# A two-layer graph network on one core: the prologue written in program order, and the softmax's reductions moved from TensorE to GpSimd

## The chip, the cores and the metric

One Trainium2 chip, one of its cores. The metric is device time in microseconds (us). On one core every run quoted here was in the fast state (mean granted TensorE clock 0.989 or more); only such runs are compared. The profiled execution's own length, the span, is some 2 us shorter than the time of the same run.

## The reference, cut to what matters

There are 32 batches of 512 nodes with 512 features, all float32.

```python
for each batch:
    h  = relu(layernorm(x))                      # layer 0
    a  = adj / max(rowsum(adj), 1e-6)
    x1 = x + relu(concat(h, a @ h) @ W.T)
    h1 = relu(layernorm(x1))                     # layer 1
    q, k = split(h1 @ Wqk);  v = h1 @ Wv
    w  = mask * rowsum(q * (adj @ (k * mask))) / sqrt(512)
    out = x1 + softmax(w over the 512 nodes)[:, None] * v
```

The softmax is over nodes, and the nodes lie on the 128 partitions (four to each), so its maximum and its sum need a reduction over partitions.

## The kernel before: the parts that the argument touches

All large products are one generator of seven block products (a Strassen scheme): each step is one group of eight matmuls of 128x256 on line 124. The names are used throughout: `y` is h times half of W, `o` the rest of layer 0, `t`, `u`, `v` the products of layer 1. A batch has 42 such groups. A group's results leave the PSUM through a copy on ScalarE and sums on VectorE. A right-hand matrix must be transposed: the rows go out to DRAM, come back exchanged in blocks (`saT`, `shT` are the tiles read back), and VectorE turns 32x32 blocks (`STREAM_TRANSPOSE`). Every engine runs its own list in order.

```python
class Softmax:                       # before; one per batch
    def maximum(self):
        ptop = ps_s.tile([1, P], F32, ...)
        nc.tensor.transpose(ptop, self.top, identity)          # over partitions, on TensorE
        nc.vector.tensor_reduce(self.ntop, ptop, AX.X, ALU.max, negate=True)
    def exponents(self):
        pbc = ps_s.tile([P, 1], F32, ...)
        nc.tensor.matmul(pbc, ones[0:1, :], self.ntop, ...)    # back to all partitions
        nc.vector.tensor_copy(self.nbc, pbc)
        nc.scalar.activation(self.e, self.w, AF.Exp, bias=self.nbc)
    def weights(self):
        psum = ps_s.tile([P, 1], F32, ...)
        nc.tensor.matmul(psum, ones, self.es, ...)             # sum over partitions
        nc.vector.reciprocal(self.rs, psum)
        ...
# the prologue: left to the scheduler, one thing after another
front_h(0)                            # batch 0: layernorm, h written to DRAM
weight_right(w0[:, F:2 * F], w2R, "w2")
turn_all(FH[0].to)                    # read back, turned on VectorE
front_a(0)                            # adj likewise
run(SINGLE[:7], [layer0_y(0)], {})
weight_right(w0[:, 0:F], w1R, "w1")
turn_all(FA[0].to)
load_x(0)                             # x of batch 0 a second time
multiply, keep = layer1_weights()     # wq, wk, wv
front_h(1); front_a(1); masks()
... # cut
with tc.manual_schedule(...):         # from here on in program order
    for i in range(B + 1):
        ...
```

Of the kernel before, what the change touches and what calls it, by code (L numbers as in the profile page):

```python
# [9 lines left out]

F32 = mybir.dt.float32
AF = mybir.ActivationFunctionType
ALU = mybir.AluOpType
# [8 lines left out]
def kernel(  # L22
# [45 lines left out]
    ps_m = ctx.enter_context(tc.tile_pool(name="ps_m", bufs=7, space=bass.MemoryType.PSUM))  # L68
    ps_s = ctx.enter_context(tc.tile_pool(name="ps_s", bufs=1, space=bass.MemoryType.PSUM))
# [117 lines left out]
    def exchange(src, name):  # L187


        t = big.tile([P, 8, P], F32, tag="s", bufs=2, name=name)  # L190
        for q in range(Q):
            nc.sync.dma_start(out=t[q * R:(q + 1) * R, :, :], in_=src[:, :, ts(q, P)].rearrange("k r j -> r k j"))
        return t
# [7 lines left out]
    ones = const.tile([P, P], F32, name="ones")  # L201
    nc.vector.memset(ones, 1.0)
# [202 lines left out]
    class Softmax:  # L405
        def __init__(self, b):
            self.b = b
            self.w = small.tile([P, C], F32, tag="w", name=f"w_{b}")
            self.e = small.tile([P, C], F32, tag="e", name=f"e_{b}")
            self.sm = small.tile([P, C], F32, tag="sm", name=f"sm_{b}")  # L410
            for n, shape in (("top", [P, 1]), ("ntop", [1, 1]), ("nbc", [P, 1]), ("es", [P, 1]), ("rs", [P, 1])):
                setattr(self, n, small.tile(shape, F32, tag=n, name=f"{n}_{b}"))
# [8 lines left out]
        def maximum(self):  # L421
            ptop = ps_s.tile([1, P], F32, tag="s", name=f"ptop_{self.b}")
            nc.tensor.transpose(ptop, self.top, identity)
            nc.vector.tensor_reduce(self.ntop, ptop, AX.X, ALU.max, negate=True)

        def exponents(self):
            pbc = ps_s.tile([P, 1], F32, tag="s", name=f"pbc_{self.b}")
            nc.tensor.matmul(pbc, ones[0:1, :], self.ntop, start=True, stop=True)  # L428
            nc.vector.tensor_copy(self.nbc, pbc)
            nc.scalar.activation(self.e, self.w, AF.Exp, bias=self.nbc)  # L430

        def row_sum(self):
            nc.vector.tensor_reduce(self.es, self.e, AX.X, ALU.add)

        def weights(self):
            psum = ps_s.tile([P, 1], F32, tag="s", name=f"psum_{self.b}")
            nc.tensor.matmul(psum, ones, self.es, start=True, stop=True)
            nc.vector.reciprocal(self.rs, psum)
            nc.vector.tensor_scalar(self.sm, self.e, self.rs, None, op0=ALU.mult)
# [17 lines left out]
    def weight_right(src, dst, name):  # L457

        s = src.rearrange("(h k r) j -> h k r j", h=2, r=R)
        for h in range(2):  # L460
            t = exchange(s[h], f"s{name}_{h}")
            for k in range(2):
                nc.vector.transpose(  # L463
                    dst[:, 2 * k + h, :, :].rearrange("p b (k r) -> p k b r", r=R),
                    t[:, :, ts(k, 2 * R)].rearrange("p k (c r) -> p k c r", r=R),
                )
        for s in right_sums(dst):
            s()

    def weight_rows(src, dst, ordered, name):  # L470


        s = src.rearrange("(h k r) j -> h k r j", h=2, r=R)
        for h in range(2):
            t = exchange(s[h], f"s{name}_{h}").rearrange("p k (a r) -> p k a r", r=R)
            if ordered:
                for q in range(2):
                    o = dst.rearrange("p a (c q r) -> p q c a r", c=C, q=Q)[:, 2 * h + q]
                    nc.vector.transpose(o, t[:, q * 4:(q + 1) * 4, :, :])
            else:  # L480
                nc.vector.transpose(dst[:, :, ts(h, H)].rearrange("p a (k r) -> p k a r", r=R), t)
# [4 lines left out]
    def masks():  # L486
        t = big.tile([P, C, 512], F32, tag="u", bufs=1, name="masks")
        mask_sb = t[:B, 0, :]
        nc.sync.dma_start(out=mask_sb, in_=nodemask)
        mask_by = t[:B, 1, :]  # L490
        nc.vector.tensor_copy(
            mask_by.rearrange("b (c q r) -> b c q r", c=C, q=Q), mask_sb.rearrange("b (q c r) -> b c q r", q=Q, c=C)
        )
        pmk = ps_s.tile([P, C, B], F32, tag="s", name="pmk")
        for c in range(C):
            nc.tensor.transpose(pmk[:, c, :], mask_by[:, ts(c, P)], identity[:B, :B])
        nc.scalar.activation(mcol, pmk, AF.Copy, scale=scale)
        nc.scalar.activation(mraw, pmk, AF.Copy)

    def layer1_weights():  # L500

        wqT = big.tile([P, C, 512], F32, tag="u", bufs=1, name="wqT")
        wkT = slots("h1T", 1, "wkT")[:, 0:4, :, :].rearrange("p s b f -> p (s b f)").rearrange("p (c f) -> p c f", c=C)
        weight_rows(wqk[:, 0:F], wqT, True, "wq")
        weight_rows(wqk[:, F:2 * F], wkT, False, "wk")
        tv = big.tile([P, C, 512], F32, tag="v", bufs=1, name="tv")
        load_rows(tv, wv)
        for c in range(C):
            nc.scalar.activation(
                vR[:, 2 * (c // 2):2 * (c // 2) + 2, c % 2, :],  # L510
                tv[:, c, :].rearrange("p (a f) -> p a f", a=2), AF.Copy,
            )
        for s in right_sums(vR):
            s()
        held = {}

        def multiply(d):
            p = held[d] = mm_tile(f"pm_{d}")
            for a in range(C):
                nc.tensor.matmul(  # L520
                    p.rearrange("p a f -> p (a f)"), wqT[:, a, ts(d, P)], wkT[:, a, :],
                    start=(a == 0), stop=(a == C - 1),
                )

        def keep(d):
            copy(mR[:, 2 * (d // 2):2 * (d // 2) + 2, d % 2, :], held[d])

        return multiply, keep

    FH, FA, F1 = {}, {}, {}  # L530

    def front_h(b):
        f = FH[b] = FrontH(b)
        f.load(0)
        f.load(1)
        for c in range(C):
            f.stats(c)
        variance(f.t)
        shift(f.t)
        for c in range(C):  # L540
            f.write(c)

    def front_a(b):
        f = FA[b] = FrontA(b)
        for h in range(2):
            f.load(h)
            f.sum(2 * h)
            f.sum(2 * h + 1)
            f.degrees(h)
            f.write(2 * h)  # L550
            f.write(2 * h + 1)

    def turn_all(t):
        for h in range(2):
            t.read(h)
            t.turn(h)
        for i in range(4):
            t.sums(i)

    front_h(0)  # L560
    weight_right(w0[:, F:2 * F], w2R, "w2")
    turn_all(FH[0].to)
    front_a(0)
    run(SINGLE[:7], [layer0_y(0)], {})
    weight_right(w0[:, 0:F], w1R, "w1")
    turn_all(FA[0].to)
    load_x(0)
    multiply, keep = layer1_weights()
    front_h(1)
    front_a(1)  # L570
    masks()
    for h in range(2):
        FA[1].to.read(h)
    if B > 2:
        FH[2] = FrontH(2)
        FH[2].load(0)
        FH[2].load(1)


    with tc.manual_schedule(  # L580
        engines={mybir.EngineType.PE, mybir.EngineType.Activation, mybir.EngineType.DVE, mybir.EngineType.SP}
    ):
        for i in range(B + 1):
# [5 lines left out]
            if i + 1 < B:  # L589
                ta, th = FA[i + 1].to, FH[i + 1].to  # L590
                at(1, ta.turn, 0)
                at(3, ta.turn, 1)
                at(3, th.read, 0)
                at(5, th.read, 1)
                for k in range(4):
                    at(4 + k, ta.sums, k)
# [12 lines left out]
            if i == 0:  # L609
                for d in range(C):  # L610
                    at(3 * d, multiply, d)
                    at(3 * d + 3, keep, d)
                for k in range(4):
                    at(13, right_sums(mR)[k])
# [24 lines left out]
            if i == B:  # L639
# [4 lines left out]
                PAIR if i < B else sorted(PAIR),  # L644
                [layer1_t(i - 1), layer1_v(i - 1)] if i > 0 else [None, None], plan,
# [9 lines left out]
            if i > 0:  # L655
                s = Softmax(i - 1)
                for n, f in ((0, s.scores), (1, s.maximum), (2, s.exponents), (3, s.row_sum), (4, s.weights)):
                    at(n, f)
                for c in range(C):
                    at(5 + c, s.apply, c)  # L660
                at(6, s.store, 0)
                at(8, s.store, 1)
# [49 lines left out]
```

## Time and profile before

| | before |
|---|---|
| time, median of the runs beside the changed kernel | 2452.25 us (2450.97 to 2453.15, 4 runs) |
| span of the profiled run | 2448.9 us |
| TensorE idle before 154 us | 69 us |
| period of a batch | 73.36 us |

From the page of the kernel before, the busy shares and the chain of work that ended last:

```profile
PE 2372.5 (97%) x10948; PEld 2070.0 (85%) x10948; DVE 1501.6 (61%) x3169; ACT 852.8 (35%) x1547; POOL 65.4 (3%) x70
PE 94%; DMA 2%; DVE 1%; ACT 1%; SPq 1%; issue 0%; POOL 0%; DVEq 0%; ACTq 0%; POOLq 0%
```

Busy and chain agree that TensorE sets the end. The TensorE timeline (start, us, engine, line, operation, out<-in; in brackets the idle time before and what ended it) shows the large idle stretches of the prologue:

```profile
23.75 3.78 PE L124 MATMUL pp_y<-w2R,hT 128*128 128x256 f32 x8 [23.75 <-DVE hT L198]
48.98 3.78 PE L124 MATMUL pp_o<-w1R,hT 128*128 128x256 f32 x8 [8.85 <-DVE w1R L463]
55.86 3.78 PE L124 MATMUL pp_o<-y,aT 128*128 128x256 f32 x8 [3.10 <-DVE aT L198]
100.00 0.60 PE L496 MATMUL pmk<-identity,masks 32*128 32x32 f32 x4 [4.91 <-DVE masks L491]
125.83 3.75 PE L124 MATMUL pp_y<-w2R,hT 128*128 128x256 f32 x8 [25.22 <-DVE rstd L227]
```

Batch 0 waits for its round trip through DRAM, then for w1, for the mask, and batch 1 for a normalization that begins only when all else has gone. A first group after a long gap takes 3.75 to 3.78 us instead of 1.89: this is called the cold clock below (in the stretch from 100 to 120 us the profile's granted TensorE clock is 0.50 of full speed).

### The profile page before, as it was taken

The numbers are of one execution on the slowest core, as the hardware profiler recorded it, in microseconds if no ns is written. First come the engines' busy times: TensorE is split into PE (matmuls) and PEld (weight loads), VectorE is DVE, ScalarE is ACT, GpSimd is POOL, SyncE is SP. The second block draws the span as 40 slices with busy tenths as digits, with TensorE's granted clock in tenths as the row PEclk, the third lists the DMA queues.
The fourth block names the chain that finished last, engine by engine and source line by source line (L and its number), as shares of the span: only waits on it lengthen the run. The fifth ranks groups of instructions, "written<-read, shape, count | busy, mean of one in ns | idle before, by whom it ended". The sixth has DMA issues, their size and how long they took to land.

```text
span 2448.9 us, 30843 instructions
## 1 busy us (share of the span) xinstructions
PE 2372.5 (97%) x10948; PEld 2070.0 (85%) x10948; DVE 1501.6 (61%) x3169; ACT 852.8 (35%) x1547; POOL 65.4 (3%) x70
## 2 busy tenths in 40 slices
PE   3599999999999999999999999999999999999998
PEld 3378888888888888888888888888888888888887
DVE  4466666666666666666666666666666666665544
ACT  2233433323433323433323433323333323333322
POOL 0000000000000000000000000000000000000000
PEclk8899999999999999999999999999999999999999
DMA  6765545655545755555656555656545655645512
GB/s 157 179 181 138 144 124 145 168 143 138 145 126 143 172 138 138 146 128 140 172 138 138 147 128 138 173 138 138 155 123 137 172 138 138 154 126 134 121 40 65
DMA packets 369930, 342.94 MB, mean 140 GB/s; under 512 B 33360, under 2 KB 270928, under 8 KB 369776
## 3 DMA queue, kind: packets, MB, share of 16 engines
q1 hardware_dynamic: 369776, 340.99, 56.2%
q8 instruction: 85, 1.39, 0.2%
q14 instruction: 69, 0.57, 0.1%
HBM read 206.64 MB, written 134.22 MB: 139 GB/s over the span
## 4 chain that ended last, share of the span: by engine, by line
PE 94%; DMA 2%; DVE 1%; ACT 1%; SPq 1%; issue 0%; POOL 0%; DVEq 0%; ACTq 0%; POOLq 0%
PE pp_o L124 17%; PE pp_y L124 9%; PE pp_t L124 9%; PE pp_u L124 9%; PE pp_v L124 9%; PE pq_o L124 9%; PE pq_y L124 5%; PE pq_t L124 5%; PE pq_u L124 5%; PE pq_v L124 4%; PE pr_o L124 4%; PE pr_u L124 2%; PE pr_t L124 2%; PE pr_v L124 2%; PE pr_y L124 2%; PE pbc L428 0%
## 5 line engine op out<-in xcount | busy, mean ns | idle before, releaser
L124 PE MATMUL pp_y<-w2R,hT 128*128 128x256 f32 x1024 | 249.0, 387 | 50.3 <-DVE rstd L227 25.2
L124 PEld LDWEIGHTS pp_y<-w2R,hT 128*128 128x128 f32 x1024 | 194.0, 192 | 77.1 <-issue 25.3
L124 PE MATMUL pp_o<-w1R,hT 128*128 128x256 f32 x1024 | 243.8, 381 | 8.8 <-DVE w1R L463 8.8
L124 PE MATMUL pp_o<-y,aT 128*128 128x256 f32 x1024 | 243.8, 381 | 3.1 <-DVE aT L198 3.1
L124 PE MATMUL pp_u<-h1m,aT 128*128 128x256 f32 x1024 | 242.4, 380 | 0.1
L124 PE MATMUL pp_v<-vR,h1T 128*128 128x256 f32 x1024 | 242.1, 379 | 0.0
L124 PE MATMUL pp_t<-mR,h1T 128*128 128x256 f32 x1024 | 241.9, 379 | 0.0
L124 PEld LDWEIGHTS pp_o<-w1R,hT 128*128 128x128 f32 x1024 | 195.7, 191 | 35.9 <-DVE w1R L463 9.2
L124 PEld LDWEIGHTS pp_o<-y,aT 128*128 128x128 f32 x1024 | 195.8, 191 | 30.4 <-DVE aT L198 3.8
L124 PEld LDWEIGHTS pp_t<-mR,h1T 128*128 128x128 f32 x1024 | 194.7, 190 | 26.3
L124 PEld LDWEIGHTS pp_u<-h1m,aT 128*128 128x128 f32 x1024 | 192.1, 190 | 29.2 <-ACT h1m L332 0.7
L124 PEld LDWEIGHTS pp_v<-vR,h1T 128*128 128x128 f32 x1024 | 194.6, 190 | 26.2
L91 ACT ACTIVATE o<-pp_o 128x512 f32<-128x512 f32 x96 | 57.3, 597 | 397.6 <-PE pp_o L124 397.6
L198 DVE STREAM_TRANSPOSE aT<-saT 128x1024 f32<-128x1024 f32 x64 | 79.7, 1245 | 151.0 <-DMA saT<-daT 141.2
L236 ACT ACTIVATE h1m<-x,nmr,rstd 128x512 f32<-128x512 f32 x128 | 100.0, 807 | 170.7 <-DVE nmr L232 170.7
L91 ACT ACTIVATE v<-pp_v 128x512 f32<-128x512 f32 x128 | 75.4, 589 | 223.6 <-PE pp_v L124 223.6
L91 ACT ACTIVATE y<-pp_y 128x512 f32<-128x512 f32 x128 | 75.8, 592 | 214.6 <-PE pp_y L124 214.6
L228 POOL TENSOR_TENSOR rstd<-rstd,mhalf 128x4 f32<-128x4 f32 x64 | 64.7, 1011 | 2318.2 <-ACT m_o L91 1187.8
L124 PE MATMUL pq_y<-w2R,hT 128*128 128x256 f32 x512 | 123.7, 384 | 1.5 <-DVE hT L85 1.5
L124 PE MATMUL pq_v<-vR,h1T 128*128 128x256 f32 x512 | 121.0, 379 | 0.0
L124 PE MATMUL pq_o<-w1R,hT 128*128 128x256 f32 x512 | 121.0, 379 | 0.0
L124 PE MATMUL pq_t<-mR,h1T 128*128 128x256 f32 x512 | 121.0, 379 | 0.0
(113 smaller groups left out, 3722.4 us busy)
## 6 DMA issues: line engine op xcount, KB each, us to landing
n<-in_x_dram SPq DMA_DIRECT2D x256, 128.0 KB, 4.8
dhT<-n SPq DMA_DIRECT2D x128, 256.0 KB, 2.1
shT<-dhT SPq DMA_DIRECT2D x256, 128.0 KB, 4.5
a<-in_adj_dram SPq DMA_DIRECT2D x256, 128.0 KB, 3.1
daT<-a SPq DMA_DIRECT2D x128, 256.0 KB, 2.5
saT<-daT SPq DMA_DIRECT2D x256, 128.0 KB, 4.5
x<-in_x_dram SPq DMA_DIRECT2D x128, 256.0 KB, 5.6
dh1T<-h1m SPq DMA_DIRECT2D x128, 256.0 KB, 2.4
```

The lines of the kernel that those rows point to most:

```text
L91: nc.scalar.activation(o, i, AF.Copy)
L124: nc.tensor.matmul(p[:, rc, :], lt[:, LEFT[k], dk, ts(rc, P)], rt[:, RIGHT[k], dk, :], start=first and n == 0, stop=True, skip_group_check ...
L198: nc.vector.transpose(o, t.rearrange("p k (c r) -> p k c r", r=R))
L228: nc.gpsimd.tensor_tensor(rstd, rstd, mhalf, op=ALU.pow)
L236: nc.scalar.activation(o, i, AF.Relu, scale=t[1][:, c:c + 1], bias=t[2][:, c:c + 1])
```

## The change

Its intent: (1) write the prologue in program order as well, load x once and the weights early into tiles that are still free, and transpose batch 0 on TensorE, which has nothing else to do there, instead of through DRAM; (2) do the softmax's two reductions on GpSimd, so that TensorE's stream has no small products in it, and give the freed PSUM bank to the large products. The diff, cut to its core:

```diff
-    ps_m = ...tile_pool(name="ps_m", bufs=7, space=PSUM)
-    ps_s = ...tile_pool(name="ps_s", bufs=1, space=PSUM)
+    ps_m = ...tile_pool(name="ps_m", bufs=8, space=PSUM)
 class Softmax:
     def maximum(self):
-        nc.tensor.transpose(ptop, self.top, identity)
-        nc.vector.tensor_reduce(self.ntop, ptop, AX.X, ALU.max, negate=True)
+        nc.gpsimd.partition_all_reduce(self.gtop, self.top, channels=P, reduce_op=ReduceOp.max)
     def exponents(self):
-        nc.tensor.matmul(pbc, ones[0:1, :], self.ntop, start=True, stop=True)
-        nc.vector.tensor_copy(self.nbc, pbc)
-        nc.scalar.activation(self.e, self.w, AF.Exp, bias=self.nbc)
+        nc.vector.tensor_scalar(self.ntop, self.gtop, -1.0, None, op0=ALU.mult)
+        nc.scalar.activation(self.e, self.w, AF.Exp, bias=self.ntop)
     def row_sum(self):
         nc.vector.tensor_reduce(self.es, self.e, AX.X, ALU.add)
+        nc.gpsimd.partition_all_reduce(self.gs, self.es, channels=P, reduce_op=ReduceOp.add)
     def weights(self):
-        nc.tensor.matmul(psum, ones, self.es, start=True, stop=True)
-        nc.vector.reciprocal(self.rs, psum)
+        nc.vector.reciprocal(self.rs, self.gs)
+def start():                                     # all of it in program order
+    load_x(0)
+    s2 = [exchange(... w2 half h ..., queue=nc.scalar) for h in range(2)]
+    fa.load(0); fa.load(1)                       # adj of batch 0
+    s1 = exchange(... w1 ..., whole("v", "sw1")) # tiles that are free until layer 1
+    fh.load(0)                                   # x of batch 1
+    sq = exchange(... wq ..., whole("u", "swq")); sk = exchange(... wk ..., slot_rows("h1m", "swk"))
+    ... statistics of x ...
+    for c in range(C):
+        normalize into v
+        turn_chunk(v, c, "h")                    # four 128x128 transposes on TensorE
+        keep_chunk(h0, c - 1, "h")               # copied out by ScalarE
+    run(SINGLE[:7], [layer0_y(0)], plan)         # adj's chunks are turned between its groups
+    run(SINGLE, [layer0_out(0)], later)
+    run(SINGLE, [None], plan)                    # the q-k weight product
+    run(PAIR, [layer0_y(1), layer1_u(0)], plan)
... # cut: positions of the steps in these plans
 with tc.manual_schedule(engines=engines):
-    for i in range(B + 1):
+    start()
+    for i in range(1, B + 1):
... # cut: for i == 1, adj of batch 2 and the sums of three right-hand matrices lie in o(1)
```

## The prediction

> **What bounds the kernel now.** I read first the page's busy shares and its chain of work that ended last: TensorE is busy 97% of the span and 94% of the chain is TensorE. So time can only be won where TensorE is idle, or where it does work that could go elsewhere. To find the idle time I asked for the busy time of each engine in stretches, cut at the points where the TensorE timeline shows a gap. Columns: stretch, its length, then busy time (and count) of TensorE matmuls, weight loads, VectorE, ScalarE, GpSimd, then granted clock, DMA share, GB/s.
>
> ```profile
> 0.00:23.75 23.75, 0.00 (x0) 0.00 (x0) 9.74 (x21) 4.21 (x5) 1.72 (x7) 1.00 0.76 181
> 23.75:40.13 16.38, 14.67 (x56) 11.62 (x56) 7.11 (x12) 4.71 (x10) 0.00 (x0) 1.00 0.32 80
> 40.13:81.19 41.06, 29.12 (x113) 24.38 (x113) 18.27 (x27) 7.84 (x15) 0.00 (x0) 0.79 0.90 193
> 81.19:125.83 44.64, 14.51 (x38) 6.43 (x36) 23.16 (x52) 12.12 (x23) 2.31 (x3) 0.70 0.68 181
> 125.83:153.83 28.00, 26.79 (x113) 22.52 (x114) 20.47 (x34) 16.63 (x32) 0.98 (x1) 0.93 0.65 180
> 153.83:2441.71 2287.88, 2287.40 (x10633) 2005.11 (x10631) 1420.73 (x3024) 806.72 (x1461) 60.40 (x60) 1.00 0.56 138
> ```
>
> Idle TensorE is 23.75 + 1.71 + 11.94 + 30.13 + 1.21 = 69 us, all before 154 us; from there to 2441.71 it never stops, at full clock, and 7 us follow it for the last store. The DMA share and GB/s of the first stretches (181 to 193 GB/s) also say that the prologue moves data nearly as fast as this kernel ever does; that matters below.
>
> In the steady part a busy TensorE is not all useful. The timeline of TensorE (start, duration, line, out<-in, count) over one softmax:
>
> ```profile
> 350.62 1.89 PE L124 MATMUL pr_y<-w2R,hT 128*128 128x256 f32 x8
> 352.35 0.27 PE L423 MATMUL ptop<-identity,top 128*1 128x128 f32 x1
> 352.45 1.89 PE L124 MATMUL pp_u<-h1m,aT 128*128 128x256 f32 x8
> 354.28 0.38 PE L428 MATMUL pbc<-ntop,ones 1*128 1x1 f32 x2
> 354.58 1.99 PE L124 MATMUL pp_y<-w2R,hT 128*128 128x256 f32 x8
> 356.42 1.89 PE L124 MATMUL pr_u<-h1m,aT 128*128 128x256 f32 x8
> 358.14 0.28 PE L437 MATMUL psum<-es,ones 128*128 128x1 f32 x2
> 358.28 1.97 PE L124 MATMUL pq_y<-w2R,hT 128*128 128x256 f32 x8
> 360.09 1.89 PE L124 MATMUL pp_u<-h1m,aT 128*128 128x256 f32 x8
> ```
>
> Undisturbed groups of eight start every 1.727 us. Here five groups take 360.09 - 350.62 = 9.47 us where 8.64 would do: the three small softmax products cost 0.83 us, mostly as breaks in the stream, not as their own duration. A second reading: the GpSimd pow of line 228 recurs every 388.60 - 315.24 = 73.36 us, while the 42 groups of a batch are 42 x 1.727 = 72.53. Both give 0.83 us a batch, and say that nothing else stops TensorE there.
>
> **What the Trainium skill says.** (1) "TensorE: Matmul & The Clock Gate", part 1, § What's actually happening: after an idle window the array runs at half clock until about 3.4 us of activity. The trace agrees: the first group after each gap takes 3.78 us in place of 1.89, so each closed gap is worth some 1.8 us more. (2) "GPSIMD Engine Reference", § 4 names GpSimd for reductions over partitions, but § 2.1 says the first call to a freshly loaded kernel pays about 6 us of code load. The order of the changed kernel shows a library instruction on GpSimd before each pair of reductions and another before the next pow; no run here shows their cost yet. (3) The same page, § 3.2, times a partition reduction of 128x2048 at 247.7 us, 0.12 us a column, so on one column only the fixed cost counts. The trace has no such instruction; its nearest, pow on 128x4, takes 1.01 us. (4) "DMA: Bandwidth & Descriptors", § Issuing engines are not separate DMA queues: ScalarE's queue shares the sixteen DMA engines with SyncE's, so the second queue for w2 adds no bandwidth. No run here shows that yet.
>
> **Part 1, softmax (steady).** Removed: 0.83 us of TensorE on each of 32 batches = 26.5 us, all on the path. Added: two reductions on GpSimd, off TensorE, but VectorE's negation and reciprocal, and ScalarE's exponential, wait for them in order. How long may one take, D? Before, in the batch at 422 us, the row maximum was ready at 422.84; nbc began at 428.05 and the reciprocal at 431.82:
>
> ```profile
> 422.68 0.16 DVE L419 TENSOR_REDUCE top<-w 128x1 f32<-128x4 f32 x1
> 428.05 0.16 DVE L429 COPY nbc<-pbc 128x1 f32<-128x1 f32 x1 [1.76 <-PE pbc L428]
> 431.82 0.17 DVE L438 RECIPROCAL rs<-psum 128x1 f32<-128x1 f32 x1 [1.54 <-PE psum L437]
> ```
>
> So VectorE already waited 5.2 us for the maximum and 9.0 us for the sum, since the products stood at fixed places in TensorE's order, and TensorE lost nothing by it. The new chain is D, negate and exponential and row sum (about 0.8), D: with 2D + 0.8 below 9.0, D under 4.1 us, it is never later than before. Estimate from pow: D is 1.5 to 4 us. The library instructions have no wait and stand right after a pow, some 22 us ahead of the maximum (13 groups), so I take them as hidden. Part 1: -26.5 us. The eighth PSUM bank gains nothing, as TensorE did not wait for banks.
>
> **Part 2, prologue.** Batch 0 of h and adj no longer goes through DRAM and back; x is loaded once; the weights' loads are issued early into tiles that are free. I walk TensorE's new order with durations of the trace.
> - Start: 1 MB of x and 1 MB of w2 share the DMA; at 190 GB/s x is complete at about 10 us (before, without w2 ahead: 7.4). Statistics 3.0, pow with its neighbours 1.4: 14.5. ScalarE then does four normalizations of 0.73 and the copies of the transposed chunks at 0.6; the last transposition is ready near 20. y(0) starts at 20, not 23.75.
> - y(0): seven groups 12.1, cold start 1.8, twelve transposes of adj at about 0.2 (a weight load of 0.19 each) 2.4: ends at 36.5, with w1 landed by 25.
> - o(0): 14 x 1.727 = 24.2, four transposes and the mask 1.2: ends at 62. Before, o(0) waited 8.85 us for w1R and 3.10 for aT.
> - The q-k weight product: 13.9 as before, its inputs landed by 40: ends at 76.
> - y(1) with u(0): hT of batch 1 must be turned by 76. Its loads end at 40, ScalarE writes it out at 54 to 58, wv's 1 MB lies in the queue between, it is read back by 68 to 70. It just fits, hidden by the weight product. So the stage begins near 76, not 125.83, and warm: it takes 24.2 plus some 2 us waiting for ScalarE (masks of h1m), so o(1) begins at about 102, not 153.83: 51 us won.
> - But then DMA traffic that before had 154 us must go in 110. Up to the half of aT(2) that VectorE wants early in o(1), I count 20.5 MiB (x of batches 0 and 1: 2; five weight blocks: 5; adj of batch 0: 1; h and adj of batches 1 and 2, loaded: 4, written out: 3.5, read back so far: 2.5; h1 of batch 0, out and back: 2; half of h 3: 0.5); at 190 to 215 GB/s that is 100 to 113 us plus the gaps. I allow 7 us of new waits in o(1) and the stage after. Part 2: -44 us.
>
> The tail is a wash: the last sum needs about 2D + 1.9 us after the last maximum, before it took 9.8.
>
> Sum: 2451.5 - 26.5 - 44 = 2381.
>
> **The rivals.** (a) A reduction that is slow or whose library load falls between maximum and exponential. Each us of D above about 5.5 then holds up ScalarE's PSUM copies and costs one to two us a batch; with 6 us of load in each batch I estimate 0.7 to 2 us a batch, 2405 to 2445, and D near 10 makes it slower than before by 100 us or more. For it: two library instructions a batch. Against it: the early position, and the 0.08 us between identity's memset and its select in the kernel before, which also has a library instruction between. (b) DMA bounds the new prologue: not 7 but 15 to 25 us of TensorE waits in the first 150 us, since VectorE runs in order and one late turn blocks the finishes behind it. Result 2390 to 2400. For it: 190 GB/s already. Against it: the plan moves some turns of batch 2 later, as if to allow for it. (c) Hardly any new wait: 2372.
>
> **Range and chances.** Faster by over 2% means under 2402.5. The middle case, (b) and (c) all stay under; only (a) reaches above it. I give (a) 13%, a fifth of that slower than 2%. So 2381, 2366 to 2408; faster 0.86, same 0.11, slower 0.03.
>
> **What would show it.** Right: pow recurs every 72.5 us in the profile after; TensorE's idle time before the first y(1) product is 20 to 25 us and that product starts at 74 to 80; o(1) ends by 135; the reductions show 1.5 to 4 us from the row maximum to the negation. Wrong: a period of 73.4 or more (part 1 fails), with ScalarE waiting for ntop longest; long idle TensorE in o(1) with VectorE waiting for saT or x (part 2 mis-sized); y(0) starting past 25 because x waited behind w2.

## The result, and the profile after

| | before | after |
|---|---|---|
| time, median | 2452.25 us (4 runs) | 2382.84 us (2381.87 to 2383.87, 4 runs) |
| ratio of fast runs | | 0.9717, 95% interval 0.9701 to 0.9734 |
| span | 2448.9 us | 2380.0 us |
| period of a batch | 73.36 us | 72.52 us |
| start of y(1) | 125.83 us | 75.24 us |
| start of y(2) | 202.17 us | 161.10 us |

Here and below, a ratio is the mean time of one kernel's fast runs over the mean of the other's in the same rounds, so it is not quite the ratio of the medians quoted. The result is correct.

The page of the kernel after, busy shares:

```profile
PE 2345.8 (99%) x10820; PEld 2056.2 (86%) x10820; DVE 1491.9 (63%) x3132; ACT 860.3 (36%) x1555; POOL 91.9 (4%) x134
```

The same cut into stretches as the prediction made for the kernel before (length, then busy time of TensorE, weight loads, VectorE, ScalarE, GpSimd; granted clock, DMA share, which as the tool counts it can pass 1, GB/s):

```profile
0.00:21.83 21.83, 4.00 (x16) 3.20 (x17) 7.81 (x18) 5.88 (x8) 1.74 (x7) 1.00 1.05 189
21.83:102.89 81.06, 77.85 (x334) 61.79 (x334) 55.32 (x103) 41.15 (x79) 3.03 (x3) 1.00 0.83 189
102.89:161.10 58.21, 51.95 (x225) 44.28 (x224) 40.09 (x85) 17.58 (x31) 2.29 (x2) 0.94 0.57 155
161.10:2373.12 2212.02, 2212.02 (x10249) 1946.93 (x10247) 1386.79 (x2927) 795.13 (x1436) 84.87 (x122) 1.00 0.55 139
2373.12:2380.00 6.88, 0.00 (x1) 0.00 (x0) 1.87 (x3) 0.60 (x1) 0.00 (x0) 0.70 0.57 152
```

TensorE is now idle 17.8 us at the start and about 9.5 us between 97 and 147 us, and never again up to 2373.12. The gaps that are left, in the TensorE timeline after:

```profile
75.24 1.89 PE L124 MATMUL pp_y<-w2R,hT 128*128 128x256 f32 x8
101.06 1.99 PE L124 MATMUL pp_u<-h1m,aT 128*128 128x256 f32 x8 [3.21 <-ACT u L91]
137.80 3.78 PE L124 MATMUL pp_t<-mR,h1T 128*128 128x256 f32 x8 [4.63 <-ACT t L91]
147.18 1.99 PE L124 MATMUL pp_v<-vR,h1T 128*128 128x256 f32 x8 [1.13 <-ACT v L91]
```

y(1) starts with no wait and on a warm clock, where it had waited 25.22 us. The new gaps all wait for a copy on ScalarE. What that copy waited for is one step back on ScalarE, whose list holds the normalization of batch 3 (`n`) just ahead of the copy of `t`:

```profile
134.34 2.93 ACT L235 ACTIVATE n<-n,nmr,rstd 128x512 f32<-128x512 f32 x4 [12.63 <-DVE nmr L231]
137.17 0.57 ACT L91 ACTIVATE t<-pp_t 128x512 f32<-128x512 f32 x1
```

and `nmr` is computed by VectorE, which had stood still twice in that stage for the halves of batch 2's adj:

```profile
113.30 1.25 DVE L199 STREAM_TRANSPOSE aT<-saT 128x1024 f32<-128x1024 f32 x1 [7.36 <-DMA saT<-daT]
126.07 1.25 DVE L199 STREAM_TRANSPOSE aT<-saT 128x1024 f32<-128x1024 f32 x1 [5.41 <-DMA saT<-daT]
```

So a name in brackets (ScalarE) is three steps from what held the work up; the experiments below take up how much each of them is worth.

The softmax. VectorE's lines after, around one of them:

```profile
379.10 0.16 DVE L418 TENSOR_REDUCE top<-w 128x1 f32<-128x4 f32 x1
379.88 0.15 DVE L424 TENSOR_SCALAR ntop<-gtop 128x1 f32<-128x1 f32 x1 [0.63 <-POOL gtop L421]
384.46 0.14 DVE L432 RECIPROCAL rs<-gs 128x1 f32<-128x1 f32 x1
```

and the GpSimd timeline after:

```profile
11.02 0.28 POOL masks.py:199 TENSOR_SCALAR_AFFINE_SELECT identity<-identity 128x128 f32<-128x128 f32 x1 [10.10 <-issue]
306.95 0.38 POOL L421 PARTITION_ALL_REDUCE gtop<-top  x1 [18.41 <-DVE top L418]
379.47 0.38 POOL L421 PARTITION_ALL_REDUCE gtop<-top  x1 [18.42 <-DVE top L418]
```

From the end of the row maximum to the negation it is 0.6 us, and from that same end to the reciprocal 5.2 us where it was 9.0. The reductions recur every 379.47 - 306.95 = 72.52 us: exactly 42 groups. The first of these lines is an oddity: a plain select stands 10.10 us after its memset (0.08 us in the kernel before). It is taken up with e3 and e6.

**Where the time came from.** Span 2448.9 - 2380.0 = 68.9 us. Of it, y(2) starts 202.17 - 161.10 = 41.1 us sooner, and 32 batches are shorter by 0.84 us, 26.9 us. The rest, about 1 us, lies in the tail and in rounding.

### The profile page after: what moved, and what is told of

The parts are those of the page before. It is cut to its first block, busy times and chain, and to the rows that moved or that the text cites. A ratio compares the mean times of both kernels' runs of the same rounds, so it can differ in the third digit from the quotient of the medians.

```text
span 2380.0 us, 30871 instructions
## 1 busy us (share of the span) xinstructions
PE 2345.8 (99%) x10820; PEld 2056.2 (86%) x10820; DVE 1491.9 (63%) x3132; ACT 860.3 (36%) x1555; POOL 91.9 (4%) x134
## 4 chain that ended last, share of the span: by engine, by line
PE 95%; DMA 2%; DVE 1%; SPq 1%; ACT 0%; issue 0%; POOL 0%; DVEq 0%; ACTq 0%; POOLq 0%
PE pp_o L124 18%; PE pp_v L124 9%; PE pp_t L124 9%; PE pp_y L124 9%; PE pp_u L124 9%; PE pq_o L124 9%; PE pq_v L124 5%; PE pq_t L124 5%; PE pq_y L124 4%; PE pq_u L124 4%; PE pr_o L124 4%; PE pr_v L124 2%; PE pr_t L124 2%; PE pr_u L124 2%; PE pr_y L124 2%; DMA x<-in_x_dram 0%
## 5 line engine op out<-in xcount | busy, mean ns | idle before, releaser
L124 PE MATMUL pp_y<-w2R,hT 128*128 128x256 f32 x1024 | 243.0, 380 | 0.0
L124 PEld LDWEIGHTS pp_y<-w2R,hT 128*128 128x128 f32 x1024 | 195.3, 191 | 27.1 <-issue 0.5
L91 ACT ACTIVATE u<-pp_u 128x512 f32<-128x512 f32 x128 | 76.2, 595 | 140.4 <-PE pp_u L124 140.4
L124 PE MATMUL pq_o<-y,aT 128*128 128x256 f32 x512 | 120.9, 379 | 0.0
```

Source lines behind the costliest of these rows:

```text
L91: nc.scalar.activation(o, i, AF.Copy)
L124: nc.tensor.matmul(p[:, rc, :], lt[:, LEFT[k], dk, ts(rc, P)], rt[:, RIGHT[k], dk, :], start=first and n == 0, stop=True, skip_group_check ...
```

## The experiments

Twelve kernels, e1 to e13 (there is no e7 on record), each with the kernel before on the same chip. "After" is 2382.84 us throughout. Kernels of different calls ran on different chips, so differences of 1 to 2 us between them mean little.

### The two parts alone

```diff
 # e1: the kernel before, with class Softmax of the kernel after
 # e2: the kernel after, with class Softmax and the 7 + 1 PSUM banks of the kernel before
```

> The kernel before with the new softmax alone (PSUM banks as before). If the two parts add up as the prediction has it, the batch period falls from 73.36 to about 72.5 us and the time by 26.5 to 27 us: about 2425 us. A second effect, seen in the profile after and not in the prediction: GpSimd's select for the identity stands 10 us behind the memset before it, after a library instruction. If that load is paid here too, the first pow, which before began at 9.2 us, begins at 11.3 and the prologue gets 2 us longer: 2427. The rival, that the GpSimd reductions cost something in the steady part that a better prologue hides, says 2435 or more.

Measured: 2425.17 us (2422.58 to 2426.28), ratio 0.9888 (0.9874 to 0.9901). That is 27.1 us less than the kernel before on that chip; the period is 72.52 us. The second effect it looked for is smaller than expected: the select came at 8.49 us, and the first pow at 9.74 in place of 9.19.

> The changed kernel with the softmax of before (three small products on TensorE, seven banks and one small one). If the parts add up: period 73.36 us again, time 2383 + 27 = 2410 us. With one library on GpSimd the identity's select should again follow its memset within 0.1 us, at about 1.0 us and not at 11. If the eighth bank mattered in the new prologue, it is longer than 2411 and the waits of TensorE before 165 us are above the 9.6 us of the changed kernel.

Measured: 2409.63 us (2407.97 to 2411.03), ratio 0.9826 (0.9812 to 0.9839), 42.65 us less than before; the period is 73.36 us. TensorE's waits between 100 and 150 us are the ones of the kernel after, within about 1 us each, so they are the prologue's own and owe nothing to GpSimd.

The parts add up: 27.1 + 42.65 = 69.8 us, against 69.4 for both together. As e2 has the old number of PSUM banks for the products and the same waits, the eighth bank shows no gain.

### What the GpSimd reduction could have cost

```diff
 # e3: one pow that waits for the row maximum, so that the library switch cannot run early
+    nc.gpsimd.tensor_tensor(self.gtop, self.top, mhalf[:, 0:1], op=ALU.pow)
     nc.gpsimd.partition_all_reduce(self.gtop, self.top, ...)
 # e4 and e5: every reduction eight times, sixteen times
-    nc.gpsimd.partition_all_reduce(...)
+    for _ in range(8):      # 16 in e5
+        nc.gpsimd.partition_all_reduce(...)
```

> The changed kernel with one more pow on GpSimd, that waits for the row maximum and stands ahead of the max reduction (its result is overwritten), so the library is switched between the maximum and its reduction, where it can't be hidden. If a switch costs the 10 us seen at the start, the negation comes about 12 us after the row maximum in place of 0.6, ScalarE's copy of u's first product comes 4 to 6 us late in each batch, and the time is 2500 to 2575 us. If a switch costs the 6 us of the Trainium skill, the negation comes at 8 us and the time is 2383 to 2400. If a switch in the steady part costs nothing (the 10 us belong to the start), the negation comes at 2 us and nothing changes.

Measured: 2391.20 us (2391.09 to 2391.53), ratio 0.9751. The GpSimd timeline of this run:

```profile
1032.00 0.55 POOL L421 TENSOR_TENSOR gtop<-top,mhalf 128x1 f32<-128x1 f32 x1 [18.30 <-DVE top L418]
1038.55 0.38 POOL L422 PARTITION_ALL_REDUCE gtop<-top  x1 [6.00 <-issue]
```

Between pow and reduction lie 6.00 us in which GpSimd waits for nothing that the profile shows: the library being exchanged. This agrees with the Trainium skill's "GPSIMD Engine Reference", § 2.1, which gives about 6 us for the first call to a freshly loaded kernel. In the kernel after the same exchange runs in the 18.4 us that GpSimd idles before the row maximum, so it is hidden, as the prediction had it. Exposed, VectorE waits for `ntop` up to 7.3 us in each batch and still the steady period is 72.52 us. The 8.4 us lost all lie at the very end, where the last batch has no next `y` and its `u` groups stand alone, so that half as many groups cover the same chain (TensorE's timeline of e3):

```profile
2345.43 3.78 PE L124 MATMUL pp_u<-h1m,aT 128*128 128x256 f32 x8 [5.13 <-ACT u L91]
2378.82 1.99 PE L124 MATMUL pq_v<-vR,h1T 128*128 128x256 f32 x8 [1.13 <-ACT m_v L91]
```

The first waits for a copy of `u` that stands, in ScalarE's list, behind the exponential of the last softmax but one; it pays the cold clock as well.

> Each reduction done eight times (the same result over again), so that one takes some 0.6 + 7 x 0.5 = 4 us. The prediction says that a reduction of up to 4.1 us is free, since VectorE already waited that long for TensorE before: same time as the changed kernel, 2383 within 0.2%, period 72.5. The rival, that any us of VectorE's waiting is paid, says up to 6 us a batch, 2400 to 2570.

Measured: 2383.70 us (2383.21 to 2384.39), ratio 0.9721: nothing lost. Eight reductions take 3.48 us, so one takes about 0.45 us from start to start.

> Each reduction done sixteen times: with the start to start time of 0.45 us that eight showed, one takes 0.6 + 15 x 0.45 = 7.3 us. The prediction put the limit near 5.5 us and the price at one to two us a batch for each us above it: 1.8 us over makes 1.8 to 3.6 us a batch, 2440 to 2500 us. The run with the exposed library load, where the maximum alone took 7 us and the steady period stayed at 72.5, speaks for a wider limit: for the maximum at least, ScalarE has slack. If both reductions are free even at 7 us, the time stays at 2383 to 2390.

Measured: 2472.97 us (2470.51 to 2473.81), ratio 1.0083 (1.0069 to 1.0096). Its GpSimd timeline, TensorE's largest group of waits (total us, times, longest), and a TensorE line:

```profile
1064.45 7.03 POOL L422 PARTITION_ALL_REDUCE gtop<-top  x16 [18.36 <-DVE top L418]
PE pq_u L124 <- ACT m_u L91: 55.6, 29, 2.2
1086.50 3.68 PE L124 MATMUL pq_u<-h1m,aT 128*128 128x256 f32 x8 [1.89 <-ACT m_u L91]
```

90 us are lost, 2.8 us a batch: some 1.9 us of waiting for a PSUM copy that stands behind late work in ScalarE's list, and in some batches, as in the line shown, the cold clock of the group after it. So a slow reduction does hurt in the way the prediction described. The three runs also show that the room is shared. The old chain took 9.0 us from maximum to sum. From the first GpSimd instruction after the maximum to the end of the last, it is 8.3 us in e3 (1032.00 to 1040.29) and 8.2 us in e4: free in the steady part. In e5 it is 15.6 us (1064.45 to 1080.00), and the excess shows. Where between 8.3 and 15.6 us the limit lies was not tried.

### What the transposes on TensorE are worth

```diff
 # e12: batch 0's h through DRAM as before; w1, n_1, wq, wk are loaded behind it
-    in-order normalization into v; turn_chunk(v, c, "h"); keep_chunk(h0, ...)
+    normalize(v, X[0][:, c, :], t, c)
+    nc.sync.dma_start(out=th0.d[c], in_=v)
+th0.read(0); th0.read(1); ... ; th0.turn(0); th0.turn(1)
```

> The kernel after, but batch 0's normalized h goes through DRAM (written, read exchanged, turned on VectorE) as it did before the change, and the loads of w1, n_1, wq and wk stand behind that in the queue; all else, the program order too, stays. Theory: in the kernel before, the round trip took 13.3 us from the shift at 10.4 to hT at 23.7; after, 5.6 us from 16.2 to 21.83. So y(0) starts some 8 us later (29 to 31), nothing later absorbs it, and the time is 2389 to 2393: the transposes on TensorE are worth about 8 of the 43 us of the prologue, and the order of the program the rest. Rival 1 (the later DMA waits of the prologue absorb it, as they did with the 3.5 us of e6): 2383 to 2386. Rival 2 (a round trip pays far more, since in program order nothing else fills the time): over 2396.

Measured: 2393.98 us (2391.63 to 2396.25), ratio 0.9758 (0.9745 to 0.9772): 11 us lost, just above the expected range. The TensorE timeline:

```profile
26.01 3.78 PE L124 MATMUL pp_y<-w2R,hT 128*128 128x256 f32 x8 [26.01 <-DVE hT L199]
```

y(0) starts only 4.2 us later, not 8, as this round trip was shorter than the one before the change. The rest came after: 2.7 us inside y(0), with the cold clock that the transposes had been warming and a wait for the second half; 1.5 us by the end of the weight product; 2.1 and 1.1 us in the two stages that follow. So of the 43 us of the prologue about 11 are lost without the transposes of h. This is not the transposes alone: the edit also puts four loads behind the round trip, and the 1.5 us are a wait for the mask, which is loaded after them (1.48 us at 52.17). Some 32 us are left by subtraction for the order, the early loads, the single load of x and the transposes of adj; these were not tried apart.

### What is left between 100 and 150 us

The kernel after still loses there 0.50 + 4.63 + 1.13 us in waits from o(1) on, plus cold groups. Six runs tried to win that back, and the start.

```diff
 # e6: w2 behind x in the same queue; a last, unused pow on GpSimd
-    exchange(... w2 ..., queue=nc.scalar)
+    exchange(... w2 ...)
+    nc.gpsimd.tensor_tensor(s.gs, s.gs, mhalf[:, 0:1], op=ALU.pow)   # the program's last GpSimd work
 # e8: batch 2's last row sums and degrees ahead of the first turn in o(1)
-    at(c - 2, FA[2].sum, c) ... plan[2].insert(0, lambda: FA[2].degrees(1))
+    at(0, FA[2].sum, c)     ... plan[1].insert(0, lambda: FA[2].degrees(1))
 # e9: e6 and e8, and the same for the first half, one stage earlier
```

> w2's loads moved from ScalarE's queue to SyncE's, behind x; and a pow that nobody reads as the last instruction of GpSimd, so that the library of pow is the one left in place at the end. If x waited for w2's packets (prediction: complete at 10 us, measured 11.5, against 7.4 in the kernel before), it is complete at 7.5 to 8 us, the first pow begins near 11 in place of 15.1, y(0) near 18 in place of 21.8, and the time falls by 3 to 4 us to 2379 (less if later waits absorb it). If x is late for another cause (four transfers of 256 KB in place of eight of 128), y(0) starts within 1 us of where it did. If the 10 us at the start are the library that the execution before left behind, the select follows its memset within 0.1 us; if they belong to any program with two libraries, it stays at 9 to 11 us.

Measured: 2380.13 us (2378.6 to 2384.58, 5 runs), ratio 0.9708 (0.9695 to 0.9721). x is complete at 7.96 us instead of 11.5, the first transposes start at 13.68 instead of 17.23, but 2.2 us of this go into a new wait for the mask, whose load did not get sooner. That wait is not a fixed price: e9, e11 and e13 below have the same program up to there, and in their profiled executions TensorE waits 0, 0 and 3.04 us for the mask. The second queue had not added bandwidth (190 GB/s over the first 21 us with it, 188 without): it had only let w2 take turns with x. This is what "DMA: Bandwidth & Descriptors", § Issuing engines are not separate DMA queues, says, now with a number. The select on GpSimd:

```profile
1.22 0.29 POOL masks.py:199 TENSOR_SCALAR_AFFINE_SELECT identity<-identity 128x128 f32<-128x128 f32 x1 [0.30 <-POOL identity masks.py:197]
```

So the 10.10 us in the kernel after were the exchange of the library that the execution before had left; ending on a pow removes it. All the profiled runs fit: 7.57 to 10.29 us where the program ends on a reduction, 0.30 where it ends on the pow, 0.08 where it has no reductions on GpSimd. It was not on the path of the kernel after, as the first pow there waited for VectorE.

> One reordering: in the first stage of the loop, the degrees of batch 2's second half before the turn of aT of batch 2, on VectorE. In the trace, VectorE stands 7.4 us before that turn for its data, ScalarE's scaled rows wait 8.4 us for the degrees behind it, their write to DRAM follows at 116 to 118 us, and the second half is turned only at 126; what VectorE does after it (normalization of batch 3) holds ScalarE and with it TensorE for 4.6 us at 133 us and again for 1.1, with a cold clock of some 2.8 us between. If this chain is the cause, the rows go out near 106, the second turn comes 6 to 8 us sooner, these waits go and the time is 2374 to 2376. If the DMA rate itself is the bound, the second half lands as late as before and the time stays at 2382 or more.

Measured: 2381.26 us (2381.11 to 2382.29), ratio 0.9711 (0.9698 to 0.9724). A miss: the second turn came 2 us sooner, the first still waited 7.63 us, and TensorE's waits stayed (3.04, 2.99, 3.93 us). The order of the degrees alone was not the cause.

> w2 behind x, the pow last, the degrees first in the loop's first stage, and the same for the first half one stage earlier (where TensorE waits 3.2 us at 98 us for ScalarE's copy of u, behind a row that waits for degrees behind a turn). If each removes its wait and they add up: 2383 - 3.5 - 8 - 3 = 2368 to 2370. If the earlier start only meets the DMA sooner, it is no better than the reordering alone, 2374.

Measured: 2378.18 us (2375.49 to 2380.86), ratio 0.9698 (0.9684 to 0.9711). That is short of both expected figures. The 3.21 us wait is gone; 5.96 us before a `t` group with the cold clock, and 1.28 us, stay, with VectorE waiting 8.11 and 3.04 us for `saT`.

```diff
 # e10 on the kernel after, e11 on e9: batch 3's loads behind both reads of batch 2's adj; first turn later
-    at2(12, f3.load, 0) ... at2(13, f3.load, 1)
+    at(3, FH[3].load, 0);   at(4, FH[3].load, 1)          # in o(1), behind ta.read(1)
-    at(1, ta.turn, 0)
+    at(1 if i > 1 else 4, ta.turn, 0)
 # e13 on e9: the loads stay; only VectorE's turns move
-    at(1, ta.turn, 0);  at(n + 2, ta.turn, 1)
+    at(1 if i > 1 else 4, ta.turn, 0);  at(3 if i > 1 else 11, ta.turn, 1)
```

> The kernel after, with two moves in the SyncE queue and one on VectorE: the loads of n_3 go out behind both reads of aT_2, and the first half of aT_2 is turned at the fifth step of o(1) instead of the second. Theory: what is left of TensorE's waits at 137.80 (4.63 us, two groups on the cold clock after it) and 147.18 (1.13 us) comes from VectorE standing still for saT_2 (7.36 and 5.41 us) because saT_2 stands in the queue behind loads that nobody wants yet; then both VectorE waits fall under 2 us, TensorE's 4.63 and most of the cold groups' 3 us go, and the time is 2374 to 2378. Rival (the 16 DMA engines are simply full there, whatever the order): n_3 arrives later by as much as saT_2 sooner, its normalization and the copy of t behind it wait just as long, 2382 to 2385.

Measured: 2381.27 us (2379.43 to 2381.84), ratio 0.9704 (0.9691 to 0.9718). 

> The three moves of the run before (w2 behind x, degrees of aT_2 first in both stages) and the one of e10. Theory: these remove different waits, so that what remains of 5.96 (with 1.8 us of cold clock) and 1.28 us of TensorE in e9 goes: 2368 to 2373. Rival (full DMA engines): 2376 to 2380, the wait only moves to another tile.

Measured: 2380.52 us (2377.12 to 2382.36), ratio 0.9702 (0.9689 to 0.9715). Both inconclusive: VectorE's wait moved from `saT` to `n` (7.79 us in e10), but the fault is partly my edit's. In the queue the loads of `n` now stood behind a read that itself waited for its rows to land in DRAM, and went out only at 117.93 us. The trace of e10 does show that the first read cannot go much sooner: its rows were sent at 101.22 us, with nothing behind them, and it went out at 108.04 us.

> e9 with nothing moved but the two turns of aT_2 on VectorE (and its sums) in o(1): the first half at the fifth step instead of the second, the second half at the twelfth instead of the eighth, behind the statistics and the shift of n_3; the loads stay where e9 has them. e10 did not decide, since its loads of n_3 stood behind a read that waited in the queue for its own rows. Theory: TensorE's 5.96 us at 131.20 in e9 is the wait for ScalarE's copy of t, which stands behind the normalization of n_3, which waits for a shift that VectorE reaches late since it stood still 8.11 and 3.04 us for saT_2 ahead of it in program order. So the two DMA waits no longer hold n_3, the 5.96 us with 1.8 us of cold clock and the 1.28 us at 140 go, and the time is 2369 to 2373. Rival (the transfers themselves set it): the waits come back at the next user of these tiles and the time is 2376 to 2380.

Measured: 2377.74 us (2377.28 to 2377.99), ratio 0.9695 (0.9682 to 0.9708). The wait before `t` is gone, as the theory said; the time is what the rival said. The time alone does not decide between them, though: this profiled execution lost time before anything that was moved, in the first line below, and began y(1) at 75.84 us where that of e9 began it at 71.55. From the start of o(1) to y(2), where the moves lie, e13 takes 56.40 us and e9 58.78: 2.4 us were won of the 9 that the theory named. On TensorE and ScalarE:

```profile
42.72 0.40 PE L622 MATMUL pmk<-identity,mask_by 32*128 32x32 f32 x4 [3.04 <-DVE mask_by L615]
139.55 3.78 PE L124 MATMUL pp_v<-vR,h1T 128*128 128x256 f32 x8 [4.85 <-ACT v L91]
138.20 0.81 ACT L235 ACTIVATE h1m<-x,nmr,rstd 128x512 f32<-128x512 f32 x1 [11.50 <-DVE nmr L231]
```

The wait has moved three groups on, to the next copy that stands behind a normalization, which waits for the next `nmr` of VectorE. VectorE's waits for data in this stage are about half of what they were, 4.22 + 1.13 us where e9 had 8.11 + 3.04:

```profile
113.24 1.25 DVE L199 STREAM_TRANSPOSE aT<-saT 128x1024 f32<-128x1024 f32 x1 [4.22 <-DMA saT<-daT]
123.50 1.25 DVE L199 STREAM_TRANSPOSE aT<-saT 128x1024 f32<-128x1024 f32 x1 [1.13 <-DMA saT<-daT]
```

Behind the first of them VectorE hardly rests (busy times of this run, columns as above):

```profile
113.24:139.53 26.29, 21.47 (x100) 18.57 (x98) 23.92 (x47) 6.04 (x10) 2.29 (x2) 0.98 0.63 169
```

VectorE is busy for 23.92 of the 26.29 us before TensorE resumes, TensorE 21.47. In this stretch VectorE is the engine with most work: it does the sums of two right-hand matrices of layer 1 (mR, vR) and of batch 0's h1T, which fall nowhere else. But from the start of o(1) at 100.01 to that `nmr` at 138.01 it is busy 32.06 us, TensorE 34.70, and its two waits, 5.35 us together, are more than the 4.85 us that TensorE loses. So work and data waits hold the `nmr` together; that VectorE's work would be the limit by itself is not shown, as no run took those sums out.

The best kernels, e9 and e13, are nominally 5 us faster than the kernel after, but their intervals overlap with its interval and they were not timed in the same rounds. They are at least not slower; more is not claimed.

## Why the prediction was right

Predicted 2381 us, measured 2382.84, inside the range. Of its signs of being right, the period (72.52 us), the start of y(1) (75.24) and the end of o(1) (127.82, by 135 predicted) came true; TensorE's idle time before y(1), 17.8 us, is below the 20 to 25 named, and the reduction's 0.6 us below the 1.5 to 4. Step by step:

- **Steady part: -26.5 us. Shown.** Period 72.52 us, and alone the part gave 27.1 us. The breaks in TensorE's stream were the cost, not the 0.27 to 0.38 us of the small products themselves.
- **A reduction is never later than the chain it replaces (break-even 4.1 us). Shown** by e4 (free at about 4 us) and e5 (slower by 2.8 us a batch at 7.3 us, against one to two us for each us above 5.5, so 1.8 to 3.6). The estimate of the duration itself, 1.5 to 4 us from the pow, was too high: 0.6 us. The break-even value itself was not tried.
- **The library exchange is hidden. Shown** by e3, which exposed its 6 us. But the price put on it in rival (a), 0.7 to 2 us a batch, was too high: nothing in the steady period, 8.4 us in all at the end. Rival (a) judged one reduction alone (about 5.5 us); the prediction's own sum, 2D + 0.8 below 9.0, is over both, and by it the 8.3 us of e3 are free.
- **The prologue's walk. Right to 2 us at every mark**: y(0) at 21.83 us (20 predicted), y(0) ends at 36.33 (36.5), o(0) at 61.51 (62), the weight product at 75.24 (76), o(1) begins at 102.89 (102). Part of this is luck: y(0) began 1.8 us late, but took 14.5 us and not 16.3, since its first group, warmed by the transposes of h, took 2.99 us and not 3.78, and four transposes of adj took 0.43 us and not 0.8.
- **New waits, 7 us in o(1) and the stage after: right in kind and place, too small.** From o(1) to y(2) the kernel after takes 58.21 us where the kernel before took 202.17 - 153.83 = 48.3, so 9.9 us were given back: 6.3 us of waits, the rest mostly groups on the cold clock after them, which the allowance had not counted. The reason given was DMA traffic, and its count holds: up to 113.30 us, where VectorE turns that half of aT(2), the DMA moved 22.0 MB (194 GB/s) for the 20.5 MiB, or 21.5 MB, that were counted. What the allowance leaves out, and rival (b) names in short, is the chain from there to TensorE: VectorE, in order, stands still for a late `saT`; its `nmr` is late; ScalarE's normalization is late; the PSUM copy behind that is late. e13 shows that with VectorE's standing still about halved, TensorE still loses 4.85 us at a later copy. Rival (b) was thus right about the mechanism and wrong in size.
- **The x load.** Predicted complete at 10 us because w2 shares the DMA; it was 11.5, and 7.96 without w2 ahead (e6). 3.5 us were there to win; e6 ended 2.7 us sooner than the kernel after, which is within the noise, and the four kernels with this move began y(1) at 71.55 to 75.84 us against 75.24, as the mask came sooner or later.
- **The tail.** A wash as predicted: 6.88 us follow the last matmul, 7.2 before.

## What to carry to other kernels

When one engine is saturated, look for breaks in its stream made by small work that another engine can do: the worth is the break (here 0.83 us a batch), and the replacement may be as slow as the waiting chain it replaces, counted over both of its steps. In a prologue, program order with early loads can win more than keeping a transposition on chip (here some 32 us by subtraction, with the transposition of adj in it, against 11). And when a wait is taken away in a stage where an in-order engine has almost no slack, it can come back at that engine's next consumer, as in e13: sum that engine's work and waits in the stage before moving anything, and compare two runs stage by stage, as a wait elsewhere can hide what a move won.

## What the Trainium skill lacked or had wrong

- "GPSIMD Engine Reference", § 2.1, has the load of about 6 us on the first call; e3 shows 6.00 us for an exchange in the steady part. It does not say that a program also pays at its start if the execution before left another library: 10.10 us in the kernel after, 7.57 in e1, 0.08 in the kernel before and in e2, which have no reductions on GpSimd.
- No page times a reduction of one column over 128 partitions: 0.38 us as shown, about 0.45 us from start to start in a row of eight (3.48 us), 0.6 us from the row maximum to its user. The figure of "GPSIMD Engine Reference", § 3.2, 247.7 us for 128x2048, says nothing of so small a one.
- "DMA: Bandwidth & Descriptors", § Issuing engines are not separate DMA queues, holds; it gives no size for the harm. A second queue with 1 MB beside the 1 MB that is wanted first delayed that by 3.5 us (11.5 against 7.96).
- "TensorE: Matmul & The Clock Gate", part 1, § What's actually happening, speaks of an idle window of about 3.4 us before the clock is halved. After 4.63 us of waiting the group took 3.78 us in place of 1.89, as it says, and after 3.21 us only 1.99. But in e6 a wait of 2.48 us was followed by a group of 2.97 us, and in e5 one of 1.89 us by a group of 3.68 and one of 2.25 us by a group of 1.99: shorter waits can be paid for too. The section also calls the window free-running, so the moment of a wait may count beside its length; no run here shows what decides it.
